# An attention and quantised-convolution kernel on one core: first stacks, first block, batch statistics and idle products rearranged

## Chip, core and metric

The kernel runs on one core of a Trainium2 chip. The metric is the device time of one execution in microseconds (us). Of the kernel before there are three runs: 2589.92, 2590.79 and 2592.28 us, median 2590.79 us. The profiled execution has a span of 2588.2 us. TensorE (PE) multiplies matrices, VectorE (DVE) and ScalarE (ACT) do the elementwise work and read PSUM, GpSimd (POOL) does small work and issues transfers, and SyncE (SP) issues transfers.

## The reference, cut to what matters

The input `x` is (4, 128, 64, 64) in float32: four images of 128 channels and 4096 pixels. Two layers follow each other.

```python
# layer 0: attention over the pixels
x_norm = group_norm(x, groups=8)                       # mean and variance of 16 channels of an image
q, k, v = split(einsum('oc,bchw->bohw', qkv_w, x_norm) + qkv_b)
attn = softmax(einsum('bhid,bhjd->bhij', q, k) * 32**-0.5)          # 4 heads of 32
x = x + einsum('oc,bchw->bohw', proj_w, attn @ v) + proj_b
# layer 1: two 3x3 convolutions with 3-bit weights and a batch norm after each
out = relu(batchnorm(conv3x3(x, lsq_quantize(w1, alpha1))))         # statistics over b, h, w
out = batchnorm(conv3x3(out, lsq_quantize(w2, alpha2)))
return relu(out + x)
```

Each batch norm needs the mean and variance of a channel over all four images. So nothing after a convolution can start before its last pixel is done.

## The kernel before

**Attention.** An image's 4096 keys are 32 steps of 128, and its queries are 8 blocks of 512, so there are 32 blocks in all. In a step, `scores` (L425) makes a 128 x 2048 tile of scores for the four heads in two pairs. The exact float32 product is had from a high and a low part of q and k that are stacked on the partitions. ACT takes the exponential (L427), `weights` (L438) multiplies by v, and DVE adds the exponentials up (L450), except for six of the 32, which POOL's accumulating transfers add (L445). The order of the work is written out by hand: the kernel is traced under a manual schedule, each engine runs its instructions in the order of the source, and `schedule` (from L594) gives each side task of a block a step. PSUM has three tiles of two banks (`pss`, tag "s") for scores and convolution tiles, and two tiles of one bank (`psa`, tag "a") for everything else. While a block runs, its `acc` holds one of these two.

**The start.** SP and ACT load image 0 in eight chunks (L567). Ahead of its loads ACT runs a one-column exponential (L112), and with it an `ACT_TABLE_LOAD`. DVE takes the statistics of each chunk (L570). `norm_parts` (from L237) goes back and forth between DVE, PE and POOL to fold the group norm into the weights `wn` and the biases `b2` and `bvn`. Then k, q and v of the first chunks are projected (`banded`, L301), split into parts by ACT (L335) and DVE (L336), and stacked. The stacks k 0 and q 0 go from SBUF to SBUF by `direct` (L385 and L387), sixteen transfers that SP and POOL issue. The other stacks go through DRAM (L340, then `load_k`, L394). The chunks left over are projected in block 0, between its steps, each in the one free `psa` tile: k 4 at step 0, q 1 at 2, v 3 at 3, k 5 at 6, and so on.

**The convolutions.** The 64 rows of an image are four bands of 16 rows, so there are 16 tiles per convolution. A tile is one `pss` tile of two banks. Half `j` of it (8 rows, 512 pixels, one bank) takes 18 products, nine taps for the high part and nine for the low part of the band (L722). `layer` says in which order the work of a tile comes:

```python
for j in range(2):
    if m >= len(done):
        conv(ready[i, b, g], ps, j, wq[i])
prepare(m)
for j in range(2):
    c = 2 * g + j
    dst = cv[b][:, c * FB : (c + 1) * FB]
    nc.vector.bn_stats(st[:, b * NB + c, :], ps[:, j, :])
    nc.scalar.copy(dst, ps[:, j, :])
```

So PE does both halves, then `prepare` lets DVE split a later band (L549 and L550, or L802 to L806), and then DVE's statistics (L774) and ACT's copy (L775) of half 0 and of half 1 follow.

The tile framework puts in the waits. It orders the accesses of different engines to one PSUM tile one after another. The first two tiles of the first convolution, `early`, are computed at the end of the attention, between the last block's closing steps. After the 16 tiles `batch_norm` (from L748) aggregates 32 chunk statistics (L751) and works out a scale and a shift. For the second convolution ACT applies them with the ReLU (L802), DVE makes the high and low part (L805, L806), and `second` prepares each band two tiles ahead. At the end DVE and ACT apply the second norm to 16 pieces of 1024 columns and SP stores them (L844 to L846).

Of the kernel before, what the change touches and what calls it, by code (L numbers as in the profile page):

```python
# [22 lines left out]
P = 128  # L23
# [55 lines left out]
def _fast_body(ctx, tc, x, norm_w, norm_b, qkv_wt, qkv_b, proj_wt, proj_b,  # L79
# [28 lines left out]
                            pattern=[[GROUP, P // GROUP], [0, GROUP]], channel_multiplier=-1)  # L108
    mhalf = const.tile([P, 1], F32, name="mhalf")
    nc.gpsimd.memset(mhalf, -0.5)  # L110
    warm = const.tile([P, 1], F32, name="warm")
    nc.scalar.activation(warm, mhalf, AF.Exp)  # L112
    ones = const.tile([P, D], F32, name="ones")
    nc.gpsimd.memset(ones, 1.0)
    worst = const.tile([P, FB // D], F32, name="worst")
# [121 lines left out]
    def norm_parts(b, st):  # L237
        mv = small.tile([P, 2], F32, name=f"mv{b}", tag="mv")
        mean = small.tile([P, 1], F32, name=f"mean{b}", tag="mean")
        dv = small.tile([P, 1], F32, name=f"dv{b}", tag="dv")  # L240
        gm = {}

        def zero():
            nc.vector.bn_aggr(mv, st.rearrange("p j s -> p (j s)"))


        def one():
            gm[0] = psa.tile([P, FB], F32, name=f"gm{b}", tag="a")
            nc.tensor.matmul(gm[0][:, 0:1], gavg, mv[:, 0:1], start=True, stop=True)

        def two():
            nc.vector.tensor_copy(mean, gm[0][:, 0:1])
            nc.vector.tensor_tensor(dv, mv[:, 0:1], mean, ALU.subtract)
            nc.vector.tensor_tensor(dv, dv, dv, ALU.mult)
            nc.vector.tensor_tensor(dv, dv, mv[:, 1:2], ALU.add)

        def three():
            gm[1] = psa.tile([P, FB], F32, name=f"gv{b}", tag="a")
            nc.tensor.matmul(gm[1][:, 0:1], gavg, dv, start=True, stop=True)

        def four():
            r = rsqrt_eps(gm[1][:, 0:1], f"gr{b}")
            a = small.tile([P, 1], F32, name=f"ga{b}", tag="ga")
            nc.vector.tensor_tensor(a, r, nw, ALU.mult)
            c = small.tile([P, 1], F32, name=f"gc{b}", tag="gc")
            nc.vector.tensor_tensor(c, mean, a, ALU.mult)
            nc.vector.tensor_tensor(c, nb, c, ALU.subtract)
            wn = wpool.tile([P, 3 * P], F32, name=f"wn{b}", tag="wn")
            nc.vector.tensor_scalar(wn, wqkv, a, None, ALU.mult)
            cb = wpool.tile([P, P], F32, name=f"cb{b}", tag="cb")  # L270
            nc.vector.tensor_copy(cb, c.to_broadcast([P, P]))
            norm[b] = [wn, c, cb]


        def five():
            wn, c, cb = norm[b]
            gm[2] = psa.tile([P, FB], F32, name=f"gb{b}", tag="a")
            nc.tensor.matmul(gm[2][:, 0:1], wqkv[:, P : 2 * P], c, start=True, stop=True)
            nc.tensor.matmul(gm[2][:, 1:2], wqkv[:, 0:P], c, start=True, stop=True)
            nc.tensor.matmul(gm[2][:, P : 2 * P], cb, wqkv[:, 2 * P : 3 * P], start=True, stop=True)  # L280

        def six():
            b2 = wpool.tile([P, 2], F32, name=f"b2_{b}", tag="b2")
            nc.vector.tensor_tensor(b2, gm[2][:, 0:2], bkq, ALU.add)
            bvn = wpool.tile([P, P], F32, name=f"bvn{b}", tag="bvn")
            nc.vector.tensor_tensor(bvn, gm[2][:, P : 2 * P], bv, ALU.add)
            norm[b] = norm[b][0], b2, bvn

        return zero, one, two, three, four, five, six

    kd, qd, vd = {}, {}, {}
    qs, ks, vs = {}, {}, {}

    def banded(out, w, x):

# [5 lines left out]
    def project_parts(b, j, xin, start=False):  # L303
# [3 lines left out]
        ps = {}  # L307

        def bank(what):
            if start:  # L310
                t = pss.tile([P, 2, FB], F32, name=f"p{what}{b}_{j}", tag="s")
                return t[:, 0, :]
            return psa.tile([P, FB], F32, name=f"p{what}{b}_{j}", tag="a")
# [61 lines left out]
    def direct(what, t):  # L375

        u = k_tile(0, 0) if what == "k" else q_tile(0, 0)
        for g in range(2):
            for s in range(4):
                i, part = divmod(s, 2)  # L380
                h = 2 * g + i
                src = t[h * D : (h + 1) * D, :, :]
                eng = (nc.sync, nc.gpsimd)[s % 2]
                if what == "k":
                    eng.dma_start(out=f32(u)[s * D : (s + 1) * D, g, :], in_=src[:, part, :])  # L385
                else:
                    eng.dma_start(out=f32(u)[s * D : (s + 1) * D, g, :, :], in_=src)  # L387
# [64 lines left out]
    def finish_parts(n):  # L452
# [30 lines left out]
        def sums_at_once():  # L483
# [3 lines left out]
            for j in range(4):  # L487
                cs = slice(j * P, (j + 1) * P)
                nc.vector.reciprocal(rc[:, cs], t["ls"][:, cs])
            weigh()  # L490
            most = [small.tile([P, 1], F32, name=f"most{i}") for i in range(2)]
            for u, m in zip((t["ls"], rc), most):
                nc.vector.tensor_reduce(m, u, AX.X, ALU.max)
# [29 lines left out]
        def store():  # L523
            nc.vector.scalar_tensor_tensor(t["x"], t["o"], bp, t["x"], ALU.add, ALU.add)
            nc.gpsimd.dma_start(out=y0[b][:, qb * FB : (qb + 1) * FB], in_=t["x"])

        return dict(copy=copy, merge=merge, sums=sums, sums_at_once=sums_at_once, spread=spread, invert=invert, gather=gather,
                    weigh=weigh, residual=residual, project=project, store=store)


# [34 lines left out]
    for j in range(NB):  # L565
        eng = (nc.sync, nc.scalar)[j % 2]
        eng.dma_start(out=halves[j // 4][:, j % 4, :], in_=x_chunk(0, j))  # L567
    st = small.tile([P, NB, 6], F32, name="st0", tag="st")
    for j in range(NB):
        nc.vector.bn_stats(st[:, j, :], halves[j // 4][:, j % 4, :])  # L570
    for f in norm_parts(0, st):
        f()

    def first_chunk(j, what, start):
        return project_parts(0, j, lambda: halves[j // 4][:, j % 4, :], start)[what]
# [2 lines left out]
        load_k(b, j)  # L578
        load_v(b, j)

    for what, j in (("k", 0), ("q", 0), ("k", 1), ("v", 0), ("k", 2), ("v", 1), ("k", 3), ("v", 2)):
        for f in first_chunk(j, what, True):
            f()
        if what == "v":
            load_k(0, j + 1)


# [6 lines left out]
    def schedule(n, before):  # L594
# [25 lines left out]
            add(slots[9], before["project"])  # L620
            add(slots[9] + 1, before["store"])
        if n + 1 < len(blocks):
            add(14, lambda: load_q(*blocks[n + 1]))
        if n == 0:
            for kt, what, j in ((0, "k", 4), (2, "q", 1), (3, "v", 3), (6, "k", 5), (9, "k", 6),
                                (12, "v", 4), (15, "k", 7), (18, "v", 5), (21, "v", 6),
                                (24, "v", 7)):
                visit((kt,), *first_chunk(j, what, False))
                if what == "k":
                    add(kt + 2, lambda j=j: load_k(0, j))  # L630
# [3 lines left out]
        if b + 1 < B:  # L634
# [10 lines left out]
            if qb == 2:  # L645
                add(slots[0], late[b][5])
                add(slots[0] + 1, late[b][6])
            chunks = {1: (), 2: (0, 1), 3: (2, 3), 4: (4,), 5: (5,), 6: (6,), 7: (7,)}
            for i, j in enumerate(chunks.get(qb, ())):
                p = project_parts(b + 1, j, lambda j=j: xin[b + 1, j])  # L650
# [89 lines left out]
    last["project"]()  # L740
    last["store"]()
    split_band(*bandlist[2])
    att.close()

    mid = ctx.enter_context(tc.tile_pool(name="mid", bufs=1))
    cv = [mid.tile([P, N], F32, name=f"cv{b}") for b in range(B)]

    def batch_norm(i, st):  # L748

        mv = small.tile([P, 2], F32, name=f"bmv{i}", tag="mv")  # L750
        nc.vector.bn_aggr(mv, st.rearrange("p j s -> p (j s)"))  # L751
        v = small.tile([P, 1], F32, name=f"bv{i}", tag="dv")
        nc.vector.tensor_scalar(v, mv[:, 1:2], alpha_s[i], alpha_s[i], ALU.mult, ALU.mult)
        r = rsqrt_eps(v, f"br{i}")
        a = small.tile([P, 1], F32, name=f"ba{i}", tag="ga")
        nc.vector.tensor_scalar(a, r, alpha_s[i], bn[i][0], ALU.mult, ALU.mult)
        c = small.tile([P, 1], F32, name=f"bc{i}", tag="gc")
        nc.vector.tensor_tensor(c, mv[:, 0:1], a, ALU.mult)
        nc.vector.tensor_tensor(c, bn[i][1], c, ALU.subtract)
        return a, c  # L760

    def layer(i, prepare, done):

        st = mid.tile([P, B * NB, 6], F32, name=f"st{i}")
        for m, (b, g) in enumerate(bandlist):
            ps = done[m] if m < len(done) else conv_tile(i, b, g)
            for j in range(2):
                if m >= len(done):
                    conv(ready[i, b, g], ps, j, wq[i])
            prepare(m)  # L770
            for j in range(2):
                c = 2 * g + j
                dst = cv[b][:, c * FB : (c + 1) * FB]
                nc.vector.bn_stats(st[:, b * NB + c, :], ps[:, j, :])  # L774
                nc.scalar.copy(dst, ps[:, j, :])  # L775
        return batch_norm(i, st)

    def count_bad():

# [33 lines left out]
            relu_rows(b, g, t, r0, r1)  # L813
        ready[1, b, g] = t["hi"], t["lo"]

    relu_band(*bandlist[0], pieces=((0, RB + 2), (RB + 2, BR + 2)))
    relu_band(*bandlist[1])


# [19 lines left out]
        load_res(B - 1, i)  # L839
    for b in range(B):  # L840
        for j in range(4):
            y = res[b, j]
            cs = slice(j * HN, (j + 1) * HN)
            nc.vector.scalar_tensor_tensor(y, cv[b][:, cs], a2, y, ALU.mult, ALU.add)  # L844
            nc.scalar.activation(y, y, AF.Relu, bias=c2)
            nc.sync.dma_start(out=out[b].rearrange("c h w -> c (h w)")[:, cs], in_=y)  # L846

# [456 lines left out]
```

## Time and profile before

| part of the page or answer | value |
|---|---|
| PE busy | 2517.2 us, 97% of the span |
| DVE busy | 2140.3 us, 83% |
| ACT busy | 2081.9 us, 80% |
| start of the first products of k (L301) | 18.68 us |
| last transfer of q 0 landed, scores go on | 31.92 us |
| `acc` of block 0 copied (L460); of block 1; of the last block | 114.81; 189.10; 2265.99 us |
| first product of the second convolution (L722) | 2415.49 us |
| first piece of the end (L844) | 2560.13 us |

The page counts PE as busy while a product is in its pipeline, so 97% does not mean that PE is at its peak. The table of 40 slices shows PE full from the second slice to the 37th. It dips once, between the two convolutions. What the ends of the kernel cost has to be read from the timeline of the first 60 us, of 2255 to 2300 us, of 2400 to 2435 us, and of the last 50 us. In a timeline a row names its start, its length, the engine, the line, and in brackets how long the engine was idle before it and who ended that.

### The profile page before, as it was taken

How to read it: one execution, taken by the hardware profiler on the slowest of the kernel's cores; microseconds unless marked ns; L12 is line 12 of the kernel's file. 1: busy time of each engine (PE TensorE's matmuls, PEld its weight loads, DVE VectorE, ACT ScalarE, POOL GpSimd, SP SyncE). 2: the span in 40 equal slices, each digit the busy share in tenths (PEclk: the TensorE clock that was granted, in tenths of full speed). 3: DMA queues.
4: the chain of work that ended last, by engine and by line, in shares of the span. 5: the costliest groups of instructions: out<-in, count | busy, mean ns of one | idle time of the engine just before them, and what ended most of it. 6: DMA issues, size and time to landing. Idle time of an engine off the chain costs nothing.

```text
span 2588.2 us, 48399 instructions
## 1 busy us (share of the span) xinstructions
PE 2517.2 (97%) x20394; PEld 1223.4 (47%) x20394; DVE 2140.3 (83%) x1402; ACT 2081.9 (80%) x2275; POOL 281.4 (11%) x456
## 2 busy tenths in 40 slices
PE   6999999999999999999999999999999999999894
PEld 3444444444444444444444444444444444477773
DVE  5898888888988898888988988888999998953344
ACT  4888899999988999999988899999889898911223
POOL 2111111111011111110011111110000000100000
PEclk9999999999999999999999999999999999999997
DMA  5876766698667767697667666986655757634004
GB/s 160 191 187 172 177 161 149 154 206 201 162 148 178 178 155 171 149 225 171 160 171 161 164 159 150 207 202 142 151 130 126 154 126 148 146 80 145 1 1 164
DMA packets 147417, 400.04 MB, mean 155 GB/s; under 512 B 59240, under 2 KB 60008, under 8 KB 118648
## 3 DMA queue, kind: packets, MB, share of 16 engines
q0 software_dynamic: 45888, 280.59, 47.9%
q1 hardware_dynamic: 100728, 115.23, 16.8%
q8 instruction: 162, 2.65, 0.4%
q10 hardware_dynamic: 576, 1.05, 0.1%
q14 instruction: 63, 0.52, 0.1%
HBM read 105.32 MB, written 55.83 MB: 62 GB/s over the span
## 4 chain that ended last, share of the span: by engine, by line
PE 88%; DVE 5%; issue 3%; DMA 2%; ACT 1%; POOL 0%; SPq 0%; DVEq 0%; POOLq 0%; ACTq 0%
PE s L425 39%; PE acc L438 34%; PE c L722 9%; DVE r L450 3%; DMA rm<-p 2%; PE l L467 1%; PE po L301 1%; PE pk L301 1%; PE pq L301 1%; PE pv L301 1%; ACT p L427 1%; DVE res L844 1%; DMA xh<-in_x_dram 0%; DMA q<-qst 0%; DVE st L570 0%
## 5 line engine op out<-in xcount | busy, mean ns | idle before, releaser
L427 ACT ACTIVATE p<-s 128x1024 f32<-128x1024 f32 x2048 | 1940.2, 1034 | 235.0 <-PE s L425 158.7
L450 DVE TENSOR_TENSOR r<-r,p 128x2048 f32<-128x2048 f32 x768 | 1758.4, 2290 | 97.3 <-ACT p L427 48.1
L425 PE MATMUL s<-q,k 64*128 64x512 f32 x8192 | 1162.3, 413 | 3.9 <-ACT p L427 2.2
L438 PE MATMUL acc<-p,v 128*32 128x512 f32 x8192 | 1021.1, 601 | 0.6 <-DVE v L355 0.6
L425 PEld LDWEIGHTS s<-q,k 64*128 64x128 f32 x8192 | 711.7, 185 | 631.9 <-issue 298.0
L438 PEld LDWEIGHTS acc<-p,v 128*32 128x32 f32 x8192 | 198.6, 109 | 453.7 <-issue 446.3
L445 POOL DMA_DIRECT2D rm<-p x160 | 138.6, 866 | 950.7 <-ACT p L427 783.6
L775 ACT COPY cv<-c 128x512 f32<-128x512 f32 x64 | 37.6, 587 | 220.8 <-DVE st L774 220.8
L722 PE MATMUL c<-hi,wq 128*128 128x512 f32 x576 | 150.1, 405 | 8.3 <-DVE hi L805 6.8
L722 PE MATMUL c<-lo,wq 128*128 128x512 f32 x576 | 148.1, 402 | 0.0
L774 DVE BATCH_NORM_STATS2 st<-c 128x6 f32<-128x512 f32 x64 | 44.7, 699 | 124.5 <-PE c L722 102.5
L722 PEld LDWEIGHTS c<-hi,wq 128*128 128x128 f32 x576 | 109.4, 191 | 40.1 <-issue 8.9
L722 PEld LDWEIGHTS c<-lo,wq 128*128 128x128 f32 x576 | 109.0, 189 | 28.9
L448 DVE TENSOR_TENSOR r<-p,p 128x2048 f32<-128x2048 f32 x32 | 73.3, 2291 | 25.0 <-ACT p L427 25.0
L336 DVE SCALAR_TENSOR_TENSOR kst<-pk,b,kst 128x512 fp32r<-128x512 f32 x32 | 24.0, 751 | 73.2 <-ACT kst L335 73.2
L336 DVE SCALAR_TENSOR_TENSOR qst<-pq,b,qst 128x512 fp32r<-128x512 f32 x32 | 24.0, 750 | 41.6 <-ACT qst L335 41.6
L471 POOL DMA_DIRECT2D r<-rm x31 | 26.3, 848 | 159.8 <-PE s L425 91.9
L340 POOL DMA_DIRECT2D qd<-qst x31 | 23.3, 753 | 177.6 <-DVE qst L336 130.2
L443 POOL DMA_DIRECT2D rm<-p x32 | 17.8, 556 | 223.3 <-ACT p L427 136.4
L335 ACT ACTIVATE kst<-pk,b 128x512 fp32r<-128x512 f32 x32 | 22.4, 701 | 21.7 <-PE pk L301 21.7
L340 POOL DMA_DIRECT2D kd<-kst x28 | 20.6, 734 | 167.6 <-DVE kst L336 159.6
L467 PE MATMUL l<-r,ones 128*32 128x256 f32 (+1 forms) x504 | 37.9, 383 | 0.5 <-issue 0.5
(129 smaller groups left out, 672.0 us busy)
## 6 DMA issues: line engine op xcount, KB each, us to landing
rm<-p POOLq DMA_DIRECT2D x192, 1024.0 KB, 7.9
q<-qd SPq DMA_DIRECT2D x248, 128.0 KB
r<-rm POOLq DMA_DIRECT2D x31, 1024.0 KB, 7.1
x<-in_x_dram SPq DMA_DIRECT2D x80, 256.0 KB
k<-kd SPq DMA_DIRECT2D x124, 128.0 KB
qd<-qst POOLq DMA_DIRECT2D x31, 512.0 KB, 6.9
kd<-kst POOLq DMA_DIRECT2D x28, 512.0 KB, 4.0
y<-x POOLq DMA_DIRECT2D x32, 256.0 KB, 5.0
```

The lines of the kernel that those rows point to most:

```text
L301: nc.tensor.matmul(out[cs, :], w[:, cs], x, start=True, stop=True)
L336: nc.vector.scalar_tensor_tensor(lo, ps[what], bias, t[:, 0, :], ALU.add, ALU.subtract)
L340: (nc.sync if start else nc.gpsimd).dma_start(out=dst[b, j].rearrange("s p n -> p s n"), in_=t)
L425: nc.tensor.matmul(s[:, i, :], k[r, half, c0 : c0 + P], q[r, half, part, :], start=(part == 0), stop=(part == 1))
L427: nc.scalar.activation(pts[step][:, 2 * half : 2 * half + 2, :], s, AF.Exp, scale=SCALE)
L438: nc.tensor.matmul(acc[n][h * D : (h + 1) * D, :], v[:, kt % KB, h * D : (h + 1) * D], pt[:, h, :], start=(kt == 0), stop=(kt == NK - 1))
L445: nc.gpsimd.dma_start(out=msum[n], in_=pt, accum_op=ALU.add)
L448: nc.vector.tensor_tensor(rsum[n], pts[step - 1], pt, ALU.add)
L450: nc.vector.tensor_tensor(rsum[n], rsum[n], pt, ALU.add)
L467: nc.tensor.matmul(t["l"][h * D : (h + 1) * D, cs], ones, r[:, h, cs], start=first, stop=end)
L722: nc.tensor.matmul(ps[:, j, :].rearrange("p (r w) -> p r w", w=W), w[:, tap, :], part[:, j * RB + kh : j * RB + kh + RB, kw : kw + W], sta ...
L774: nc.vector.bn_stats(st[:, b * NB + c, :], ps[:, j, :])
```

## The change

It has five parts. (1) ACT issues its loads before it loads its table. (2) `keep_warm` adds products of a constant with itself whose result nobody reads: 26 during the loads, 3 and 6 within the group norm, and 10 after each convolution. (3) The group norm uses fewer DVE instructions (`c` and the biases change sign for it), and the product for `bvn` moves behind q. (4) The transfers of stack 0 are dealt to the queues in another order, q also to ACT's; v 3 is projected before block 0, and the chunks within block 0 stand three steps apart. (5) In a convolution, the statistics and the copy of half 0 stand ahead of the products of half 1, the statistics of the first 30 chunks are aggregated during the last tile, `batch_norm` has its constants worked out ahead, the high part of the first band is written by ACT directly, `bounds` (the maxima of the last block) moves behind the splitting of band 2, and the first piece of the end is cut in two.

```diff
-    warm = const.tile([P, 1], F32, name="warm")
-    nc.scalar.activation(warm, mhalf, AF.Exp)
...
         def two():
+            nc.vector.tensor_tensor(dv, mv[:, 0:1], gm[0][:, 0:1], ALU.subtract)
+            nc.vector.scalar_tensor_tensor(dv, dv, dv, mv[:, 1:2], ALU.mult, ALU.add)
             nc.vector.tensor_copy(mean, gm[0][:, 0:1])
-            nc.vector.tensor_tensor(dv, mv[:, 0:1], mean, ALU.subtract)
-            nc.vector.tensor_tensor(dv, dv, dv, ALU.mult)
-            nc.vector.tensor_tensor(dv, dv, mv[:, 1:2], ALU.add)
...
-            nc.tensor.matmul(gm[2][:, P : 2 * P], cb, wqkv[:, 2 * P : 3 * P], start=True, stop=True)
+        def five_v():
+            gm[3] = psa.tile([P, FB], F32, name=f"gw{b}", tag="a")
+            nc.tensor.matmul(gm[3][:, 0:P], norm[b][2], wqkv[:, 2 * P : 3 * P], start=True, stop=True)
...
+    def keep_warm(count):
+        t = psa.tile([P, FB], F32, name=f"idle{count}", tag="a")
+        for _ in range(count):
+            nc.tensor.matmul(t[:, 0:P], gavg, gavg, start=True, stop=True)
...
     def direct(what, t):
+        engines = (nc.sync, nc.gpsimd) if what == "k" else (nc.scalar, nc.sync, nc.gpsimd)
-            for s in range(4):
+            for c, s in enumerate((0, 2, 1, 3)):
-                eng = (nc.sync, nc.gpsimd)[s % 2]
+                eng = engines[(4 * g + c) % len(engines)]
...
+    nc.scalar.activation(table, mhalf, AF.Exp)
+    keep_warm(26)
...
-    for f in norm_parts(0, st):
-        f()
+    zero, one, two, three, four, five, six, five_v, six_v = norm_parts(0, st)
+    zero()
+    one()
+    keep_warm(3)
+    two()
+    three()
+    keep_warm(6)
+    four()
+    five()
+    six()
...
-            for kt, what, j in ((0, "k", 4), (2, "q", 1), (3, "v", 3), (6, "k", 5), (9, "k", 6),
-                                (12, "v", 4), (15, "k", 7), (18, "v", 5), (21, "v", 6),
-                                (24, "v", 7)):
+            for kt, what, j in ((0, "k", 4), (3, "k", 5), (6, "v", 4), (9, "k", 6), (12, "v", 5),
+                                (15, "k", 7), (18, "q", 1), (21, "v", 6), (24, "v", 7)):
...
     split_band(*bandlist[2])
+    last["bounds"]()
...
+        end = mid.tile([P, 15], F32, name=f"end{i}")
+        nc.gpsimd.memset(end[:, 0:1], float((B * NB - 2) * FB))
         for m, (b, g) in enumerate(bandlist):
             ps = done[m] if m < len(done) else conv_tile(i, b, g)
+            if m == len(bandlist) - 1:
+                nc.vector.bn_aggr(end[:, 1:3], st.rearrange("p j s -> p (j s)")[:, : 6 * B * NB - 12])
+                nc.vector.tensor_scalar(end[:, 2:3], end[:, 2:3], float((B * NB - 2) * FB), None, ALU.mult)
             for j in range(2):
                 if m >= len(done):
                     conv(ready[i, b, g], ps, j, wq[i])
-            prepare(m)
-            for j in range(2):
+                if j == (0 if m < len(done) else 1):
+                    prepare(m)
                 c = 2 * g + j
-                dst = cv[b][:, c * FB : (c + 1) * FB]
-                nc.vector.bn_stats(st[:, b * NB + c, :], ps[:, j, :])
-                nc.scalar.copy(dst, ps[:, j, :])
-        return batch_norm(i, st)
+                if m == len(bandlist) - 1:
+                    nc.vector.bn_stats(end[:, 3 + 6 * j : 9 + 6 * j], ps[:, j, :])
+                else:
+                    nc.vector.bn_stats(st[:, b * NB + c, :], ps[:, j, :])
+                nc.scalar.copy(cv[b][:, c * FB : (c + 1) * FB], ps[:, j, :])
+        keep_warm(10)
+        return batch_norm(i, end)
...
+        for dst in (hi_inner.bitcast(F32R), t["inner"][0]):
+            nc.scalar.activation(dst[:, a - lo_row : e - lo_row, :],
+                                 cv[b0].rearrange("p (h w) -> p h w", w=W)[:, a:e, :], AF.Relu,
+                                 bias=c1, scale=a1)
...
+            for p in range(2 if b == j == 0 else 1):
+                n = HN // 2 if b == j == 0 else HN
```

## Prediction

> **What bounds the kernel now.** I read the chain first, then the groups, and then the timeline of four places.
>
> ```profile
> PE 88%; DVE 5%; issue 3%; DMA 2%; ACT 1%; POOL 0%; SPq 0%; DVEq 0%; POOLq 0%; ACTq 0%
> ...
> L775 ACT COPY cv<-c 128x512 f32<-128x512 f32 x64 | 37.6, 587 | 220.8 <-DVE st L774 220.8
> L722 PE MATMUL c<-hi,wq 128*128 128x512 f32 x576 | 150.1, 405 | 8.3 <-DVE hi L805 6.8
> L722 PE MATMUL c<-lo,wq 128*128 128x512 f32 x576 | 148.1, 402 | 0.0
> L774 DVE BATCH_NORM_STATS2 st<-c 128x6 f32<-128x512 f32 x64 | 44.7, 699 | 124.5 <-PE c L722 102.5
> ```
>
> PE carries 88% of the chain. The 1152 convolution products wait 8.3 us in all, and 6.8 of that is one gap, between the convolutions. Within a convolution PE never stops: 18 products take 4.28 us, a tile 8.6 us. The statistics (0.70 us) and copies (0.59 us) follow in the shadow of the next tile. The copies wait for the statistics all 64 times, 220.8 us, which costs nothing today.
>
> The timeline at the end of the first convolution shows how the readers of one tile follow each other:
>
> ```profile
> 2406.40 2.31 PE L722 MATMUL c<-lo,wq 128*128 128x512 f32 x9
> 2408.75 0.70 DVE L774 BATCH_NORM_STATS2 st<-c 128x6 f32<-128x512 f32 x1 [6.56 <-PE c L722]
> 2409.49 0.58 ACT L775 COPY cv<-c 128x512 f32<-128x512 f32 x1 [6.67 <-DVE st L774]
> 2410.10 0.70 DVE L774 BATCH_NORM_STATS2 st<-c 128x6 f32<-128x512 f32 x1 [0.65 <-ACT cv L775]
> ...
> 2413.87 4.06 ACT L802 ACTIVATE t<-cv,bc,ba 128x576 f32<-128x576 f32 x4 [2.45 <-DVE bc L759]
> ...
> 2415.49 4.18 PE L722 MATMUL c<-hi,wq 128*128 128x512 f32 x9 [6.77 <-DVE hi L805]
> ```
>
> DVE's statistics of half 1 wait for ACT's copy of half 0, although the halves are different banks and both only read. The order of accesses holds for the whole tile of two banks.
>
> The waits of PE in block 0, and the chain of the start:
>
> ```profile
> PE pv L301 <- DVE qst L336: 2.4, 1, 2.4
> PE pq L301 <- DVE kst L336: 1.5, 1, 1.5
> ...
> PE acc L438 <- DVE v L355: 0.6, 1, 0.6
> ```
> ```profile
> 18.75 1.91 PE pk L301 x16
> ...
> 25.87 5.91 DMA q<-qst
> ```
>
> In block 0 PE waits for a chunk's reader, because one `psa` tile is all that the chunks have. Before it, the last transfer of q 0 is issued at 25.87 us and lands at 31.78.
>
> **What the Trainium skill says.** "TensorE: Matmul & The Clock Gate", Part 1: PE's clock falls to half after an idle window of about 3.4 us and returns after as long a busy one. The trace agrees: after the gap of 6.77 us the first 9 products took 4.18 us instead of 2.31, and at the start a k chunk took 1.94 us, later 1.05. "PSUM — Partial Sum Buffer", Specifications: ScalarE and VectorE can access PSUM in parallel at full bandwidth when no bank collides. So the wait above is the program's, not the chip's; no run here shows the two reading at once. "DMA: Bandwidth & Descriptors", Issuing engines are not separate DMA queues: more issuers save issue time only. The trace agrees so far that SP needs about 0.6 us per q issue.
>
> **The change part by part.**
>
> *Half 0 read ahead of half 1.* In the changed program as built, the first product of half 1 of each tile waits for ACT's copy of half 0, which waits for DVE's statistics of it. Before, it had no wait. The tile is one object, so the write of bank 1 is ordered behind the reads of bank 0. Cost per tile from the timeline above: without a wait the next product would follow the nine at 2406.40 + 2.14 (the step of a group of nine) = 2408.54. The chain of statistics and copy lets the next one in at 2410.10. That is 1.56 us, during which the 18 products of half 1, and behind them every later tile, stand in PE's queue. DVE and ACT are free then, since `prepare` comes after half 1 is queued. It happens in 14 tiles of the first convolution (two are `early`) and 16 of the second: 30 x 1.56 = **+46.8**. If a stall hides 0.15 of it or adds as much, 42 to 51. A stall of 1.6 us is too short to lose the clock.
>
> *Tile 2 of the first convolution* stalls longer, for its statistics queue behind what DVE now has ahead. Lo of band 2 ends at 2289.3. Then `bounds` (1.66, 2281.32 to 2282.98 in the trace), six column products at 0.19 (1.1), statistics-copy-statistics of `early` tile 0 (2.0), hi and lo of band 3 (2.1), the same of `early` tile 1 (2.0), statistics (0.7) and copy (0.6) of tile 2: 2299.5. PE ends half 0 at 2287.93 + 4.28 = 2292.2. The stall is 7.3 instead of 1.56: **+5.8**, and the clock falls: **+2.2** (18 cold products, 2415.49 to 2422.02, 6.53 instead of 4.28). In the first tile of the second convolution the statistics queue behind hi and lo of the second band: **+1.0**. Together 6 to 12.
>
> *The start.* ACT issues its loads 1.1 us sooner, but transfers are busy at 0.8 to 1.0 from 2 to 10 us, and the 26 idle products end at about 12.8 (an idle product costs about 0.64 cold like row L280, 0.32 warm), as the statistics do: −0.8, between 0 and 1.7. Warm group-norm products −0.5, gb −0.4, its `bvn` product off the path −0.6, DVE operations −0.4. The 3 and 6 idle products are longer than the gaps they fill, +0.9. Warm k and q −1.8 (two rows of 1.94 become 1.05). So q is ready 3.6 us earlier. Issue over three queues starts the last transfer some 3.7 earlier, and its landing is nearer the 4.7 of POOL's rows than 5.9. In all **−4.3**, 3 to 6.5.
>
> *Block 0.* The spacing removes 1.5 + 2.4 + 0.6, and the half clock after them (12 score products at 48.50 took 2.93 instead of 1.66, with v 3 about 1.5). v 3 moves to a time when PE waits anyway: 0.9. **−6.9**. New: the parts of k 5 wait for the store of k 4, three steps earlier instead of six. If that store is late, ACT holds the exponentials for up to 2 us. So 4 to 8.
>
> *Between the convolutions* (6.8 us from last to first product). Aggregating 15 numbers instead of 192 (1.02 becomes about 0.25), three DVE operations fewer (0.6), one statistics-copy pair fewer after the last product (1.35), high part without DVE (0.5): −3.2. Ten idle products fill the 3.6 us that remain: no cold clock, −2.2. **−5.4**.
>
> *The end.* The same shorter chain without ACT's part: **−2.4**. The cut of the first piece gives 0.1, as 405 GB/s of stores bound the rest.
>
> Edits in blocks 1 to 31 (group norm of the next images) lie behind exponentials and cost nothing; gw waits for b2, which DVE ends (197.8) as PE gets there.
>
> Sum: +46.8 + 9.0 − 4.3 − 6.9 − 5.4 − 2.4 = **+36.8**, 2627.6 us.
>
> **The rivals.** (A) *The stall is hidden:* half 1 starts as before, and only the savings remain: −19.0, 2572 us. For it speaks that hardware does not need the wait, against it that the program has it and that statistics already wait in this way 32 times. Chance 0.05. (B) *The statistics queue behind hi and lo in every tile* (2.1 us more): 30 x 2.1 = +63, 2690 us. Against it: DVE's order has hi and lo right after half 0's statistics, done long before the next half ends. In the second convolution they wait for ACT's ReLU first, which also fits. Chance 0.06. (C) *The start and block 0 give a third* (the loads bound the start, store of k 4 late): +7, 2635. Chance 0.15. The main case has 0.74.
>
> **How the numbers follow.** Likeliest 2627.5. Least case: stalls 42, the rest +6, savings 25: 2614. Worst: 51 + 12 − 13: 2641. C lies inside; A and B stay out with 0.11, so 2611 to 2642. Faster only through A: 0.05; same 0.01; slower 0.94.
>
> **What would show it.** Right: products of `c` with 30 waits for ACT's copy of 1.4 to 1.6 us, one of about 7; a tile every 10.2 us; first scores before 28 us; copy of block 0 near 103; first product of the second convolution 3.6 after the last of the first. Wrong: no wait in L722's row beyond the gap, or waits above 3 us.

## The result, and the profile after

The changed kernel takes 2634.71 us, the median of four runs from 2634.39 to 2635.89. The kernel before, on the same chip, takes 2590.85 (2589.92 to 2592.28). The ratio is 1.017 with a 95% interval of 1.0152 to 1.0187, so the change costs 44 us. The forecast was 2627.5, between 2611 and 2642.

The two profiled executions have spans of 2588.2 and 2632.7. Cut at events that both timelines show, the 44.5 us between them lie here. The last column gives the terms of the prediction, sorted into the same stages.

| stage | before | after | change | predicted |
|---|---|---|---|---|
| to the aggregation of the statistics of x (`mv`) | 13.05 | 11.88 | −1.2 | −0.8 |
| from there to the scores that follow the first products of `acc` | 23.20 | 23.20 | 0.0 | −3.5 |
| rest of block 0, to the copy of its `acc` | 78.6 | 71.7 | −6.8 | −6.9 |
| blocks 1 to 31, to the first product of `c` | 2151.1 | 2150.3 | −0.8 | 0 |
| first convolution, first to last product | 142.8 | 173.9 | +31.0 | +29.8 |
| last product to the first of the second convolution | 6.8 | 3.6 | −3.2 | −3.2 |
| second convolution | 139.8 | 167.1 | +27.3 | +23.8 |
| the end | 32.9 | 31.1 | −1.9 | −2.4 |

The groups of the page that answer to those shown of the kernel before (busy us, mean ns of one, then the idle time of the engine just before them):

```profile
L823 ACT COPY cv<-c 128x512 f32<-128x512 f32 x64 | 37.5, 587 | 274.4 <-DVE st L822 256.2
...
L751 PE MATMUL c<-hi,wq 128*128 128x512 f32 x576 | 154.7, 413 | 51.8 <-ACT cv L823 48.8
L822 DVE BATCH_NORM_STATS2 st<-c 128x6 f32<-128x512 f32 x60 | 41.8, 698 | 157.7 <-PE c L751 156.1
...
L751 PE MATMUL c<-lo,wq 128*128 128x512 f32 x576 | 148.2, 401 | 0.0
```

The products of `c` had waited 8.3 us in all; now it is 51.8, nearly all for ACT's copies. A statistic, a copy and a product of lo cost what they did: 0.70, 0.59 and 0.40 us. So no operation became dearer; an order became one that waits.

The waits of PE in the convolutions alone, as us in total, number, longest:

```profile
PE c L751 <- ACT cv L823: 48.8, 30, 6.8
PE c L751 <- DVE hi L562: 1.6, 1, 1.6
PE c L751 <- issue: 1.4, 1, 1.4
```

There are thirty waits, one of 6.8, one of 2.4 and 28 of about 1.41 (48.8 − 6.8 − 2.4 = 39.6). One of the 28 in the timeline, from half 1 of one tile to half 1 of the next:

```profile
2416.11 2.40 PE L751 MATMUL c<-hi,wq 128*128 128x512 f32 x9 [1.41 <-ACT cv L823]
...
2422.66 2.30 PE L751 MATMUL c<-lo,wq 128*128 128x512 f32 x9
...
2425.00 0.70 DVE L820 BATCH_NORM_STATS2 end<-c 128x6 f32<-128x512 f32 x1 [2.35 <-PE c L751]
2425.73 0.59 ACT L823 COPY cv<-c 128x512 f32<-128x512 f32 x1 [3.65 <-DVE end L820]
...
2426.37 2.41 PE L751 MATMUL c<-hi,wq 128*128 128x512 f32 x9 [1.41 <-ACT cv L823]
```

Half 0 ends, DVE takes its statistics, ACT copies it, and only then does PE go on with half 1. The reader should see two things. DVE (2.35 idle) and ACT (3.65 idle) were free and waiting, so no queue is in this. And the tile takes 2426.37 − 2416.11 = 10.26 us where it took 8.60: 1.66 lost, not 1.41. The bracket counts from the modelled end of the last product, 0.17 after the next group could have begun (2.31 − 2.14). And the first group after a wait takes 2.24 instead of 2.14 to the start of the next.

The long wait is that of tile 2 of the first convolution:

```profile
2282.99 0.70 DVE L822 BATCH_NORM_STATS2 st<-c 128x6 f32<-128x512 f32 x1 [0.25 <-issue]
...
2287.11 0.69 DVE L822 BATCH_NORM_STATS2 st<-c 128x6 f32<-128x512 f32 x1
...
2288.51 1.30 DVE L822 BATCH_NORM_STATS2 st<-c 128x6 f32<-128x512 f32 x2 [0.71 <-ACT cv L823]
2289.24 1.18 ACT L823 COPY cv<-c 128x512 f32<-128x512 f32 x2 [0.77 <-DVE st L822]
...
2290.47 4.21 PE L751 MATMUL c<-hi,wq 128*128 128x512 f32 x9 [6.78 <-ACT cv L823]
```

With one more at 2284.39, left out here, these are five statistics: two of each early tile, and only then that of tile 2, the second of the two in the row of 2288.51. PE ended half 0 at 2283.7 and waits. After it nine products take 4.21 us instead of 2.31: the clock fell.

In block 0 the waits for a chunk's reader are gone. PE's waits from 25 to 110 us:

```profile
PE s L435 <- DMA q<-qst: 1.2, 1, 1.2
PE pv L310 <- DVE v L364: 1.0, 2, 0.8
PE acc L448 <- DVE v L364: 0.5, 1, 0.5
...
```

The two waits of `pv` lie before block 0, at 25.86 and 27.12, where v 2 and v 3 are projected. The 0.5 us for v was 0.6 before.

### The profile page after: what moved, and what is told of

Same layout as the page of the kernel before. It is cut to its first block, busy times and chain, and to the rows that moved or that the text cites. A ratio compares the mean times of both kernels' runs of the same rounds, so it can differ in the third digit from the quotient of the medians.

```text
span 2632.7 us, 48667 instructions
## 1 busy us (share of the span) xinstructions
PE 2537.2 (96%) x20504; PEld 1232.2 (47%) x20504; DVE 2138.9 (81%) x1401; ACT 2083.8 (79%) x2278; POOL 280.4 (11%) x459
## 5 line engine op out<-in xcount | busy, mean ns | idle before, releaser
L751 PE MATMUL c<-hi,wq 128*128 128x512 f32 x576 | 154.7, 413 | 51.8 <-ACT cv L823 48.8
L310 PE MATMUL po<-av,wp 128*32 128x512 f32 x256 | 33.4, 594 | 4.4 <-DVE av L526 4.4
```

The costliest lines, as they stand in the source:

```text
L751: nc.tensor.matmul(ps[:, j, :].rearrange("p (r w) -> p r w", w=W), w[:, tap, :], part[:, j * RB + kh : j * RB + kh + RB, kw : kw + W], sta ...
```

## The experiments

**The theories.** O: the tile of `c` is one object of two banks, so products of half 1 are ordered behind the readers of half 0; this order costs the time. Q: statistics, copies and preparation now stand elsewhere in the queues of DVE and ACT, or PSUM is read beside a running product, and that costs the time. R: the waits hide behind something else, and the start or block 0 cost it. All kernels below compute the whole result. The kernels that were compared on one chip share runs of the kernel before: 2592.22 us for the first four, 2590.53 for the next four, 2591.21 for the last.

### The order of before put back

```diff
             for j in range(2):
                 if m >= len(done):
                     conv(ready[i, b, g], ps, j, wq[i])
-                if j == (0 if m < len(done) else 1):
-                    prepare(m)
+            prepare(m)
+            for j in range(2):
                 c = 2 * g + j
```

> The changed kernel, with only the loop over a tile of a convolution put back: products of both halves, then the preparation of later bands, then statistics and copies of both halves; all else of the change stays. Theory O (the wait of half 1 for the copy of half 0 costs the time): the profile of the changed kernel has the first convolution 31.0 us longer than before and the second 27.3 + 2.25 longer (2.25 for the warm clock it starts with). This goes; the statistics and the copy of half 0 come back into the two chains behind the last product, 2 x 1.35. 2634.7 - 60.6 + 2.7 = 2577, up to 2579 if the ten idle products no longer keep the clock up over a gap that is 1.35 longer. No wait of c for an ACT copy is left. Rival R (start and block 0 or the columns ahead of the convolutions cost the time, the waits hide behind something else): 2620 or more.

Measured: 2577.96 us, 0.9944 times the kernel before (0.9928 to 0.9961). PE's waits in the convolutions:

```profile
PE c L751 <- POOL t L550: 2.6, 1, 2.6
PE c L751 <- DVE hi L562: 1.6, 1, 1.6
```

Thirty waits and some 57 us are gone, and what is left of the change is faster than the kernel before. R falls. The gap to the second convolution is 2.6 behind the idle products instead of 1.4, as the statistics and the copy of half 0 are back in its chain, and the clock did not hold over it: the first 18 products took 5.87 us (2408.36 to 2414.23) instead of 4.38.

### The new order alone, in the kernel before

```diff
                     conv(ready[i, b, g], ps, j, wq[i])
-            prepare(m)
-            for j in range(2):
+                if j == (0 if m < len(done) else 1):
+                    prepare(m)
```

> The kernel before, with only the new order in the loop over a tile: half 0 is read ahead of the products of half 1. Theory O: 30 waits; a tile takes 10.26 instead of 8.6 us in the profile of the changed kernel, so 30 x 1.67 = 50; tile 2 waits some 2.5 longer, without the bounds and column products that the changed kernel has ahead of it; the first tile of the second convolution 1 to 2.4; less 2 x 1.35 in the chains behind the last products. 2590.9 + 50 + 2.5 + 2 - 2.7 = 2643, between 2639 and 2646. Rival R (the waits hide, other parts cost the time): 2588 to 2600.

Measured: 2645.98 us, 1.0207 times the kernel before (1.019 to 1.0224), so 53.8 us more where 52 were expected.

```profile
PE c L722 <- ACT cv L775: 46.2, 30, 5.1
PE c L722 <- DVE hi L805: 5.5, 1, 5.5
PE c L722 <- DVE hi L549: 1.6, 1, 1.6
```

The same thirty waits, made by two moved lines. This edit alone costs more than the whole change. But O and Q both say so: it moves the readers too.

### The new order, with the halves apart

```diff
-            ps = done[m] if m < len(done) else conv_tile(i, b, g)
+            ps = done[m] if m < len(done) else None
...
                 if m >= len(done):
+                    ps = pss.tile([P, 2, FB], F32, name=f"c{i}_{b}_{g}_{j}", tag="s")
                     conv(ready[i, b, g], ps, j, wq[i])
```

> The changed kernel with its order of statements, but each half of a tile from tile 2 on is a PSUM tile of its own (one of the same three buffers, of which it uses one bank), so that nothing orders the products of half 1 behind the readers of half 0. Theory O, the order over the whole tile is the cause: the waits of c for the copy of the half just ended go, a half waits for the copy of the half three earlier, which is long done, except that half 1 of tile 2 waits for the readers of an early tile (about 2 us). 2634.7 - 60.6 + 2 = 2576, 2573 to 2579. Rival Q, the new place of statistics and copies in the queues of DVE and ACT costs the time (hi and lo of later bands late, PSUM read while PE writes beside it): the order is unchanged, so 2625 to 2636, or products slower than 2.15 us per nine.

Measured: 2577.41 us, 0.9946 (0.993 to 0.9963).

```profile
PE c L751 <- ACT cv L824: 2.1, 1, 2.1
PE c L751 <- DVE hi L562: 1.6, 1, 1.6
PE c L751 <- issue: 1.3, 1, 1.3
```

```profile
2397.25 2.31 PE L751 MATMUL c<-lo,wq 128*128 128x512 f32 x9
...
2399.40 2.30 PE L751 MATMUL c<-hi,wq 128*128 128x512 f32 x9
2399.60 0.70 DVE L821 BATCH_NORM_STATS2 end<-c 128x6 f32<-128x512 f32 x1 [2.43 <-PE c L751]
2400.33 0.59 ACT L824 COPY cv<-c 128x512 f32<-128x512 f32 x1 [3.73 <-DVE end L821]
...
2401.54 2.31 PE L751 MATMUL c<-lo,wq 128*128 128x512 f32 x9
```

The statements stand in the order of the changed kernel, half 0 is read while half 1 is multiplied, and groups of nine follow each other in 2.14 to 2.15 us. So neither the place of the readers in their queues nor reading one bank beside a product into another costs anything that shows: Q falls, O holds. The two halves now lie in different buffers; products into the second bank of a buffer beside a reader of its first bank were not run. "PSUM — Partial Sum Buffer", Specifications, of the Trainium skill says that ScalarE and VectorE can read PSUM in parallel at full bandwidth if no bank collides. No run here shows those two at once; what this one shows is that DVE and ACT each read one bank in 0.70 and 0.59 us while PE wrote another, as fast as before. The one long wait left is that of tile 2, expected at 2 and measured at 2.1.

### Bounds and columns where DVE is idle

`last["bounds"]()` and the loop for `a_q`, `a_g` and `a_n` move to stand right after `last["sums_at_once"]()`.

> The changed kernel with the bounds (1.66 us of DVE) and the six column products (about 1.0) put where DVE waits for the last projection (it is idle there for 5.05 us), not ahead of the statistics of the early tiles. As the prediction has it, the wait of tile 2 is a queue on DVE: it falls from 6.78 to about 4.1, and the time by 2.7, to 2632; if the clock stays up through the shorter wait, by 2.2 more, to 2630. Rival (tile 2 waits for the load of its band or for the readers of the early tiles alone, which would start no sooner): 2634.5 and a wait of 6 to 7 us.

Measured: 2632.82 us, 1.0157 (1.014 to 1.0174), where the changed kernel has 1.017.

```profile
2282.78 0.70 DVE L822 BATCH_NORM_STATS2 st<-c 128x6 f32<-128x512 f32 x1 [0.92 <-DMA y<-x]
...
2290.28 3.92 PE L751 MATMUL c<-hi,wq 128*128 128x512 f32 x9 [5.24 <-ACT cv L823]
```

The wait falls from 6.78 to 5.24, 1.5 instead of 2.7. So the queue on DVE was a part of it, and the rival, a wait of 6 to 7 us, falls. But the readers of the early tiles could not start as soon as DVE was free. Between lo of band 2 and the first statistics of an early tile the changed kernel's DVE took 2.47 us (2280.52 to 2282.99). Here 0.92 of this is left, as idle time that the store of the last sum with x ends. 2.47 − 0.92 is the 1.5 that came off. The kernel before has the same wait, where the prediction's sum goes straight from lo of band 2, which ends at 2289.31, to DVE's next work:

```profile
2290.07 0.70 DVE L774 BATCH_NORM_STATS2 st<-c 128x6 f32<-128x512 f32 x1 [0.76 <-DMA y<-x]
```

The time of one run can't show 1.5 us: the 31 blocks from the first copy of `acc` to the last took between 2150.4 and 2154.4 in ten profiles (the two kernels and the first eight experiments), with nearly the same program in them. The last section shows one source of this scatter.

### Both repairs

The halves apart, and bounds and columns ahead.

> The changed kernel with both repairs: the halves of a tile as PSUM tiles of their own, and bounds and column products where DVE waits for the last projection. If the 2.05 that half 1 of tile 2 still waits with the halves apart is the queue on DVE ahead of the early tiles' readers (1.66 + 1.0), it goes: some 2 us under the halves apart alone, about 1.0066 times less than before, 2574 where before is 2591. If it is the readers themselves, the wait of 2 stays and the time is that of the halves apart.

Measured: 2574.81 us, 0.9943 (0.9927 to 0.996). The wait of half 1 of tile 2 falls from 2.1 to 0.5. What fell away was the queue on DVE, as the prediction has it; but the time can't be told from that of the halves apart alone (0.9946).

### No idle products

All four calls of `keep_warm` are left out of the kernel with both repairs.

> Both repairs, and no idle products anywhere: not the 26, 3 and 6 at the start, not the 10 after each convolution. Clock theory of the prediction: the first 18 products of the second convolution take 6.4 to 6.5 instead of 4.5 (2 us lost). At the start the prediction counts on the idle products for warm k, q and group-norm products (1.8 + 0.5, less 0.9). Counter theory from the traces: the clock was down again before the group norm came, so the 3 and 6 ran cold and only delayed it. Then, counted from the aggregation of the statistics of x, the first k is evacuated at 6.5 instead of 7.5 us, the low part of q starts at about 8.9 instead of 9.07, and the first full group of scores at 17.5 to 17.9 instead of 17.9. If the idle products earn what the prediction says: 8.5 or more, 10.5 or more, 19.5 or more.

Measured: 2578.59 us in one run. At the second convolution:

```profile
2407.46 3.88 PE L748 MATMUL c<-hi,wq 128*128 128x512 f32 x9 [3.54 <-issue]
2411.19 2.31 PE L748 MATMUL c<-lo,wq 128*128 128x512 f32 x9
```

The gap is the same, 3.5 us, and the 18 products take 5.87 instead of the 4.37 of the kernel with both repairs: the ten idle products earn 1.5 us, where 2 were expected. The start is another story. Four windows of the changed kernel, with the busy time of PE and of its weight loads, then DVE, ACT and POOL, then the granted clock, the share of the DMA engines and GB/s:

```profile
10.00:12.00 2.00, 0.00 (x0) 0.00 (x0) 1.41 (x3) 0.00 (x0) 1.03 (x2) 0.93 0.04 4
12.00:14.00 2.00, 1.69 (x8) 1.69 (x9) 0.70 (x4) 0.00 (x0) 0.00 (x0) 0.50 0.01 0
14.00:16.00 2.00, 2.00 (x11) 2.00 (x11) 0.57 (x4) 0.00 (x0) 0.56 (x1) 0.50 0.00 0
16.00:18.00 2.00, 2.00 (x15) 1.99 (x18) 0.43 (x2) 0.00 (x0) 0.00 (x0) 0.50 0.03 8
```

The 26 idle products, two passes each:

```profile
1.89 7.50 PE L303 MATMUL idle<-gavg 128*128 128x128 f32 x52 [1.89 <-POOL mhalf L110]
```

They ended at 9.39, the first product of the group norm came at 12.31, and by then the clock was at half. So the 3 and the 6 ran cold, 2.91 us for the 6, and the products with `c` (row `gb`), whose input was there at 15.97, began at 17.16. Without any idle product they come sooner. Counted from the aggregation, in us:

| | products `gb` | first k evacuated | low part of q | scores after first `acc` |
|---|---|---|---|---|
| before | 4.05 | 7.64 | 10.07 | 23.20 |
| changed kernel | 5.28 | 7.48 | 9.07 | 23.20 |
| no idle products | 3.57 | 6.51 | 8.94 | 22.40 |
| longer idle (below) | 3.27 | 4.94 | 6.52 | 20.49 |

The counter theory's 6.5 and 8.9 are met, and the first full group of scores came at 17.10, even before its 17.5; the prediction's 8.5 and 10.5 are not met. In the changed kernel's run the idle products of the start earned less than nothing. The same holds with the order of before put back and with the halves apart: the 26 ended at 9.9 and 10.0, the aggregation came at 12.33 and 13.15, the clock was at half for the group norm, and the scores came at 23.27 and 22.80. In the kernel with the columns ahead and in that with both repairs the 26 took 8.40 and 8.67 us instead of 7.50, so they ended at 10.3 and 10.6; the aggregation came at 11.69 and 11.78, the clock lasted into the group norm, and the scores came at 21.91 and 21.65. What the 26 earn hangs on the gap between their end and the landing of x, and both move from run to run.

### Idle products up to the group norm

```diff
-    keep_warm(26)
+    keep_warm(36)
...
-    keep_warm(6)
+    keep_warm(4)
```

> Both repairs, and idle products that reach to the group norm: 36 instead of 26 ahead of it, 4 instead of 6 ahead of its last products. If the clock is what was missing at the start: no half clock between 2 us and the first scores; from the aggregation of the statistics of x, the first k is evacuated at about 5.1 instead of 7.5 us, the low part of q starts at 6.7 instead of 9.07 and the first full group of scores comes at 15.5 instead of 17.9; 2.4 off the time. If transfers of q and k bound the first scores whatever comes before them: 17 to 18, and no gain.

Measured: 2574.14 us, 0.9935 (0.9919 to 0.9952).

```profile
12.00:14.00 2.00, 2.00 (x19) 1.95 (x18) 0.89 (x6) 0.00 (x0) 0.00 (x0) 1.00 0.01 0
14.00:16.00 2.00, 1.68 (x16) 1.48 (x20) 0.99 (x5) 0.00 (x0) 0.56 (x1) 1.00 0.00 0
16.00:18.00 2.00, 2.00 (x34) 1.07 (x34) 0.39 (x2) 0.78 (x2) 0.00 (x0) 1.00 0.04 8
```

The clock stays up, k is evacuated at 4.94 (expected 5.1), the low part of q starts at 6.52 (6.7), the first full group of scores comes at 15.22 (15.5), and the scores after the first `acc` come 2.7 sooner than in the changed kernel. So the start was clock-bound, and the transfers move along with what comes before them. The time moves less than the trace: 2574.14 against 2574.81 with 26 and 6, which can't be told apart. The profile of the latter is one of those in which the clock lasted, so that only 1.2 us lie between the two there (20.49 and 21.65).

### Two issuers for q, and no cut at the end

```diff
-        engines = (nc.sync, nc.gpsimd) if what == "k" else (nc.scalar, nc.sync, nc.gpsimd)
+        engines = (nc.sync, nc.gpsimd)
...
-            for p in range(2 if b == j == 0 else 1):
-                n = HN // 2 if b == j == 0 else HN
+            for p in range(1):
+                n = HN
```

> Both repairs, and two small parts of the change undone at places far apart in time. (1) k 0 and q 0 are issued by SP and POOL alone, not q by ACT, SP and POOL. By the prediction the third issuer starts the last transfer of q some 2 us earlier than two would, so the first full group of scores falls from 17.9 us after the aggregation of the statistics of x to 18.7 or more later. Counter theory: the sixteen DMA engines are busy to 0.9 from the first transfer of k to the last of q, so the issuer doesn't matter: 17.6 to 18.2. (2) The first piece of the end is not cut in two. By the prediction the cut gains 0.1. Counter theory: the first stores then run dry (375, 209 and 169 GB/s in three slices, instead of 400), and from the first sum of the end to the last byte it takes 28.57 with the cut and 28.07 without, so that the cut gives nothing or costs up to 0.5.

Measured: 2580.37 us in one run.

```profile
30.53 5.06 PE L435 MATMUL s<-q,k 64*128 64x512 f32 x20 [2.75 <-DMA q<-qst]
```

In the changed kernel, with three issuers:

```profile
28.13 0.49 PE L435 MATMUL s<-q,k 64*128 64x512 f32 x1
...
29.80 2.57 PE L435 MATMUL s<-q,k 64*128 64x512 f32 x15 [1.17 <-DMA q<-qst]
```

The scores that wait for the last of q start 30.53 − 12.57 = 17.96 after the aggregation. With three issuers it is 17.92 in the changed kernel, 17.98 with the order put back and 18.04 with the halves apart. So the third issuer brings q no sooner, as "DMA: Bandwidth & Descriptors", Issuing engines are not separate DMA queues, of the Trainium skill has it: the transfers share the same engines (share 0.93 and 0.94 from 24 to 28 us in this run). The counter theory's number holds, the prediction's step does not. Another difference stands in this profile. PE has no score to do before the last of q and idles 2.75 us in one piece, and its 20 scores take 5.06 us at half clock, where 19 took 3.3 in the changed kernel. So the scores after the first `acc` come at 25.48, not 23.20. Whether the third issuer is what spares the others this is not shown by one run.

The end, from the first sum to the end of the span, took 28.42 here without the cut, 28.07 in the kernel before and 28.77 with the new order alone; with the cut it took 28.57 in the changed kernel, 28.6 with the columns ahead, and 27.55 to 27.86 in the five others of the first eight. The cut may give some 0.4; the scatter is as large, so this stays open.

### The last wait of tile 2

In the kernel with the longer idle products, `split_band(*bandlist[2])` moves ahead of `last["project"]()`.

> Halves apart, bounds and columns ahead, idle products to the group norm (36, 3, 4), and one edit more: hi and lo of band 2 are made ahead of the last projection, while DVE waits for it, so that the products of tile 2 need not wait for hi (1.56 us in every profile so far). If that wait is the queue on DVE (hi stands behind the last sum with x), it goes: 1.6 under the kernel with the longer idle products, which had 0.9935 of the time before, so 0.9929, about 2572.5 where before is 2591. If the load of band 2 or a buffer makes it wait, 2574 as that kernel.

Measured: 2574.82 us, 0.9933 (0.992 to 0.9947).

```profile
2279.75 0.70 DVE L823 BATCH_NORM_STATS2 st<-c 128x6 f32<-128x512 f32 x1 [3.04 <-DMA y<-x]
...
2282.51 2.41 PE L751 MATMUL c<-hi,wq 128*128 128x512 f32 x9 [2.15 <-ACT cv L824]
```

The wait for hi (1.56) is gone, and the wait of half 1 is back at 2.15 instead of 0.5: PE merely reached it sooner. What holds it now is the first statistics of the early tile, 3.04 us idle until the store of the last sum with x lands. `st` is a tile of the pool `mid`, which is opened where the attention's pools were closed. That its first write waits because of this is read from the program and was not tried by a run. So the expected 1.6 turned into another wait. This and the kernel with longer idle products are the best measured, and not to be told apart.

## Why the prediction was right, and where its sizes were off

**The main term** was right in mechanism. The steps "the tile is one object, so the write of bank 1 is ordered behind the reads of bank 0" and "DVE and ACT are free then" are shown by the halves apart and by the idle times in the timeline. The rivals fell: A (the stall is hidden, 2572) names the time without the wait, which the repaired kernels reach; B's queue (waits above 3 us in every tile) isn't there. The number of C, 2635, is the one measured, but by coincidence: block 0 gave what the main case said, the store of k 4 was in time, and the start fell short through the clock and not through the loads. The size of the main term was a little small. An ordinary tile loses 1.66, not 1.56, since a group that follows a wait takes 0.1 longer; on 28 tiles that is 2.8 us.

The profiles differ by 44.5 us where the sum has 36.8. Of the 7.7 between, 3.1 lie at the start, 4.7 in the two convolutions (2.8 of them the 0.1 of each of 28 waits, 1.6 a clock that fell, below) and 0.5 at the end, and the 31 blocks took 0.8 off. So two of the signs named ahead were missed, both by the start: the first score came at 28.13 and not before 28, and block 0 was copied at 106.83 and not near 103.

**Tile 2** was forecast at 7.3 + 2.2. From the step of 2.14 after the last group (2281.38 + 2.14 = 2283.52) to 2290.47 it is 6.95, and 18 products took 6.50 instead of 4.28, so 2.2 for the clock. That 1.5 of it is DVE's queue of bounds and columns, the runs with both ahead confirm; that moving them takes off 2.7, they refute, since the store of the last sum is the next to hold the readers.

**The first tile of the second convolution** waited as forecast (2.61 where 1.56 + 1.0 was predicted), but the clock fell after it, which the prediction had not counted:

```profile
2440.89 0.59 ACT L823 COPY cv<-c 128x512 f32<-128x512 f32 x1 [3.01 <-DVE st L822]
...
2441.53 3.85 PE L751 MATMUL c<-hi,wq 128*128 128x512 f32 x9 [2.42 <-ACT cv L823]
```

Its 18 products took 5.90 instead of 4.28, which costs 1.6. So what the ten idle products saved at the gap (1.5 by the run without them, 2.2 by the prediction), the wait right behind it lost again. The trace of the kernel before had a warning. In block 0 a wait about as long as the one forecast here was followed by the half clock, which the prediction counts there:

```profile
47.33 1.25 PE L301 MATMUL pv<-wn,xh 128*32 128x128 f32 x32 [2.38 <-DVE qst L336]
48.50 2.93 PE L425 MATMUL s<-q,k 64*128 64x512 f32 x12
```

**The start** is the term that was mis-sized: −1.2 in place of −4.3. The loads seem to have given what was said (−1.2 for −0.8), but one pair of profiles can't show it: the aggregation came at 13.05 and 13.78 in the two kernels with the old order of loads, and between 11.69 and 13.15 in the nine with the new one. The step that failed is "the 26 idle products end at about 12.8", from 0.64 us for a cold and 0.32 for a warm one. They ended at 9.39: a warm one takes 0.24 (ten, of two passes each, in 2.39 us between the convolutions), a cold one 0.45 to 0.54. With it "warm group-norm products" fell: counted from the aggregation, the first product of k began at 6.07 us where it had been 5.63, though the sum has it 1.0 sooner. "Warm k and q" gave 1.4 of its 1.8. So q was ready 2.2 us earlier and not 3.6, and 1.2 of that is the earlier aggregation. With the products reaching to the group norm, the mechanism works as the prediction described it. A second step failed beside it: "issue over three queues starts the last transfer some 3.7 earlier". The last issue ended at 25.98 instead of 27.51, 1.5 sooner, and the last of q came 0.95 sooner against the aggregation (17.92 for 18.87); with two issuers it came at 17.96. The first exponentials, though, came 1.25 later (18.65 for 17.40). The third issuer is not shown to be the cause: with it they came between 17.11 and 18.73 in five other profiles with 26 idle products or none, and with two issuers at 19.42. Why they came later in the changed kernel stays open. In all nothing was left of the gain at the first `acc`.

**Block 0** gave 6.8 for 6.9. This stretch took between 71.7 and 71.8 us in the eight of the ten profiles that have its new schedule, and 78.6 and 78.7 in the two without. The store of k 4 was in time.

**Between the convolutions** the gap is 3.6 as forecast. **The end** gave 1.9 for 2.4: the first sum comes 2.4 sooner after the last product, and the stores behind it took 0.5 longer, which is within the scatter shown above.

## What to carry to other kernels

Reading part of a multi-bank PSUM tile while the rest was still to be written put the readers on the critical path here, though the banks differ: make each part that is read early a tile of its own. Work that is to shorten a chain once should be done once; here a shorter chain behind two last tiles was bought with thirty waits. Idle products must reach to the next real work, and their number should be counted from a duration in the trace, not from a look-alike product; where the gap moves from run to run, they must reach to its longest. Here the profiles in which 26 stopped short were slower up to the first `acc` (22.80 to 23.27 with three issuers) than the one with none (22.40).

## What was not expected of the hardware

- Between 1.8 and 2.5 us the length of a wait did not decide whether the clock fell. Near 1912 us PE waits ahead of the same projection (`po`) in every one of the eleven profiles, for 2.40 to 2.52 us. In eight of them the clock fell behind it, in three it stayed up (the changed kernel, the halves apart, both repairs). The halves apart, and then the longer idle products:

```profile
1915.37 1.06 PE L310 MATMUL po<-av,wp 128*32 128x512 f32 x8 [2.48 <-DVE av L526]
1916.36 1.66 PE L435 MATMUL s<-q,k 64*128 64x512 f32 x12
```
```profile
1911.56 1.46 PE L310 MATMUL po<-av,wp 128*32 128x512 f32 x8 [2.48 <-DVE av L526]
1912.95 2.82 PE L435 MATMUL s<-q,k 64*128 64x512 f32 x12
```

- The three profiles in which it stayed up have the three shortest stretches of 31 blocks (2150.4 to 2151.1; the others 2151.2 to 2154.4), so this is a part of the scatter between runs. Without idle products one wait of 1.82 us, at 167.29, was enough; waits of 2.05 and 2.15 us in tile 2 and 28 waits of 1.41 were not. "TensorE: Matmul & The Clock Gate", Part 1, of the Trainium skill speaks of idle windows of about 3.4 us on a free-running clock; the measured waits are shorter, and that equal waits differ would fit a window that runs free.
- In the clock records of the eleven profiles each stretch at half clock, apart from the one after the last product, lasts 3.41 or 6.83 us.
- In the changed kernel the clock was down 2.3 us after PE went idle at 9.39 (clock 0.93 in the window from 10 to 12), and in the kernel with the columns ahead 3.3 us after, in spite of 1.5 us of products in between. At half clock it took some 6 us of nearly unbroken idle and group-norm products until it was full again (12.3 to 18.6).
- The profile's clock reads 1.00 before its first change. In the kernel before the windows of the start show 1.00 while a chunk of k takes 1.94 us, twice its warm 1.05: the row isn't proof of a warm array until it has changed once.
